# Two mixture layers on one core: the branch of rare blocks ahead of the sure ones, and the last sure blocks added to the residual by one-hot matrices

## The chip, the core and the metric

The kernel is one program on one core of a Trainium2 chip. The core has five engines that run their own instruction streams and meet at semaphores: PE multiplies matrices (PEld is its weight load), DVE and ACT do element-wise work, POOL issues indirect DMAs here, and SP issues most of the plain ones. The metric is device time in microseconds (us) of one execution, lower is better, as the median of several runs. Before the change: median 962.89 us of 3 runs (954.0, 962.89 and 962.95).

## The reference

A residual stream of 1024 tokens with 256 features goes through four layers, each an attention and a feed-forward part, each gated and added to the stream. All is fp32. The two feed-forward parts that matter are mixtures of experts. That of layer 0 takes 6 of 16 experts for each token, and adds a shared expert:

```python
probs = softmax(xf @ gate_w.T)                    # xf: [1024, 256], 16 experts
_, idx = top_k(probs + gate_b, 6)
cw = einsum('tk,tke->te', take(probs, idx), one_hot(idx, 16))
for W1, B1, W2, B2, W3, B3, c in experts:         # H = 176
    h = silu(xf @ W1.T + B1) * (xf @ W3.T + B3)
    y = y + c[:, None] * (h @ W2.T + B2)
z = silu(xf @ ws1.T + bs1) * (xf @ ws3.T + bs3) @ ws2.T + bs2
return y + z
```

Layer 3 does the like with 2 of 8 experts, 512 wide and without bias. The feed-forward part of layer 1 uses weights rounded to three values, for which a mean over the whole weight is needed first:

```python
scale = mean(abs(w))
w_q = sign(w) * (abs(w) >= scale * 0.7)           # w1 [1024, 256], w2 [256, 1024]
```

## The kernel before

The stream lies in SBUF as eight tiles of 128 rows (`stream`, `x[t]`). The parts follow one another: `attention0`, `ffn0`, `attention1`, `ffn1` and so on; a scheduler orders the instructions of each engine along the dependencies and the program's order, and an engine runs its own in that order.

**Blocks.** In `ffn0` and `ffn3` the routing sorts tokens by expert on the chip, into blocks of 128 rows that belong to one expert. The worst case has `NB0` = 63 blocks in layer 0 and `NB3` = 23 in layer 3; 55 and 20 (`SURE0`, `SURE3`) are always run, the others stand in a branch, `tc.If(used > sure)`, on a number that the routing leaves in SBUF. In the profiled execution the branch was not entered. Ahead of it, `keep_rows` (L371) writes the stream to a DRAM buffer `sums`, so that blocks can add to it there; layer 0 has two such buffers, for even and odd blocks (the second holds only what is added), layer 3 has one.

**One block**, by the lines of the profile:

- `fetch`, L1174: POOL issues an indirect DMA that gathers the block's rows, with their expert weights, from DRAM (`xd`) into `xs`. Six such tiles exist, and the gathers run four blocks ahead.
- `turn`, L1186: PE transposes the rows, DVE copies them out (L1187), DVE picks the weight of the expert (L1192), and PE's sequencer reads the offset of the expert's weights into a register (L1202, `value_load`, some three instructions).
- `up`: L1211 and L1215 in layer 0 (bias, then gate and up projection), L1226 in layer 3; ACT does the silu (L1234), DVE the product (L1235).
- `turn_hidden`: transposes on PE (L1241), copy on ACT (L1243).
- `down`, L1250: the down projection; ACT or DVE copies the result into `ring` (L1261, L1259), and POOL issues an indirect DMA (L1262) that adds the 128 rows to `sums`.

The three stages of neighbouring blocks are interleaved: step `i` turns block `i`, does `up` of `i - 1` and `down` of `i - 2`. After each step of layer 0, `between(i)` places other work: the folding of attention 1's weights (`fold1`, at every third step until it ends), then steps of `ternary1` (from step 33), which make the three-valued weights of layer 1: absolute sums on DVE (L1493), a PE sum over partitions, the threshold, and two DVE passes over each eighth of the weights (L1512, L1513).

**After the blocks** of layer 0, SP (L1403) and ACT (L1405) load both buffers back, 512 KB at a time, DVE adds them (L1408), and `attention1` begins: layernorm (L394 writes `xn`), transposes (L406), projections (L421), then softmax from L427. After layer 3's blocks, four DRAM-to-DRAM DMAs (L1662) copy `sums` to the output, two from SP and two from ACT. These are the lines around the branch and the end of layer 0:

```python
def run(self, sure):
    self.blocks(0, sure, self.between)
    used = nc.values_load(self.used, min_val=0, max_val=self.nb)
    with tc.If(used > sure):
        self.blocks(sure, self.nb, lambda i: None)
```

## Time and profile before

| what | value |
|---|---|
| median of 3 runs | 962.89 us (954.0 to 962.95) |
| the profiled execution | 967.09 us, its span 965.3 us |
| mean granted PE clock in it | 0.941 |
| PE busy | 856.9 us, 89% of the span |
| DVE, ACT, POOL busy | 509.9, 286.8, 345.7 us |
| layer 0, 272 to 451 us: PE busy | 171.44 of 179 us |
| 451 to 479 us: PE busy | 0.10 of 28 us |
| layer 3, 835 to 950 us: PE busy | 114.53 of 115 us |
| 950 to 965.3 us: PE busy | 2.13 of 15.3 us |
| scatters of layer 0 (L1262) | 55, median 1592 ns |
| gathers of layer 0 (L1174) | 55, median 987 ns |

The span runs from the first to the last instruction, and the execution's time has 1.8 us around it. A row of a group gives the line, the engine, the operation, the tile written and the tiles read, and how often; times in brackets are how long the engine had been idle and what released it. An fp32 matmul of the program appears as two records on PE. "PEq", "POOLq" and "SPq" are the sequencers, whose loads, branches and DMA issues do not count as busy time. A DMA row of POOL shows the issue alone; the data land later.

### The profile page before, as it was taken

The page shows a single profiled execution, that of the slowest core. Times are in us where ns is not written, and L with a number is a line of the kernel's source. Part 1 is how long each engine was busy: PE and PEld are TensorE (multiplying, and loading weights), DVE is VectorE, ACT ScalarE, POOL GpSimd, SP SyncE. Part 2 cuts the span into 40 slices and gives each one's busy share as a digit, 9 for nine tenths or more (in the row PEclk, how much of TensorE's full clock was granted, in tenths as well). Part 3 has the DMA queues.
Part 4 walks back from the last instruction along what each step waited for, and adds up shares of the span by engine and source line. Part 5 has one row for each costly group of instructions (what it writes and reads, how often), then busy time and mean ns, then how long its engine had stood idle before and what let it go on. Part 6 is the DMA issues. An engine that isn't in the chain of part 4 may idle for free.

```text
span 965.3 us, 12724 instructions
## 1 busy us (share of the span) xinstructions
PE 856.9 (89%) x4467; PEld 555.5 (58%) x4467; DVE 509.9 (53%) x1299; ACT 286.8 (30%) x559; POOL 345.7 (36%) x262
## 2 busy tenths in 40 slices
PE   6999999999999999986199986997867889999994
PEld 4444336876667876764046872754544556666662
DVE  4566648748624444571427755867776856222220
ACT  2122014433112322322113445415534441122221
POOL 1454543110146787786001323402311302144421
PEclk9999999999779999998599999986988999999998
DMA  9201157000256666655640000360000012122223
GB/s 364 79 21 34 61 160 200 22 22 9 84 129 158 125 141 150 121 82 63 186 174 1 1 1 0 111 227 1 1 22 1 1 44 54 43 45 45 39 23 66
DMA packets 38762, 75.15 MB, mean 78 GB/s; under 512 B 6240, under 2 KB 26706, under 8 KB 37322
## 3 DMA queue, kind: packets, MB, share of 16 engines
q1 hardware_dynamic: 23562, 52.01, 16.0%
q0 software_dynamic: 14496, 20.47, 13.1%
q10 hardware_dynamic: 640, 1.84, 0.5%
q8 instruction: 39, 0.64, 0.3%
q14 instruction: 25, 0.20, 0.1%
HBM read 58.73 MB, written 16.61 MB: 78 GB/s over the span
## 4 chain that ended last, share of the span: by engine, by line
PE 31%; DVE 10%; issue 4%; ACT 3%; POOL 2%; DMA 0%; POOLq 0%; ACTq 0%; DVEq 0%
PE wide L1226 7%; PE mm L421 5%; PE mm L1250 3%; PE wide L1436 2%; PE mm L451 2%; PE mm L656 2%; PE mm L965 2%; PE wide L923 1%; PE mm L1457 1%; DVE mx L934 1%; DVE attn L936 1%; PE mm L1637 1%; PE mm L1241 1%; DVE big L1483 1%; POOL h L1482 1%
## 5 line engine op out<-in xcount | busy, mean ns | idle before, releaser
L437 POOL TENSOR_TENSOR attn<-attn,sm 128x1024 f32<-128x1024 f32 x32 | 60.9, 1903 | 212.5 <-DVE sm L436 192.5
L1235 DVE SCALAR_TENSOR_TENSOR blk<-wide,weight,blk 128x176 f32<-128x176 f32 (+1 forms) x75 | 37.0, 493 | 135.3 <-ACT blk L1234 121.2
L1262 POOL DMA_INDIRECT sums<-ring,big x55 | 88.1, 1601 | 33.6 <-issue 10.2
L421 PE MATMUL wide<-xT,big 128*128 128x512 f32 x192 | 86.7, 600 | 0.3 <-ACT big L556 0.3
L683 DVE TENSOR_TENSOR rope<-wide,big 128x512 f32<-128x512 f32 x96 | 59.6, 683 | 47.7 <-PE wide L421 46.6
L1174 POOL DMA_INDIRECT xs<-xd,big x55 | 54.9, 999 | 63.3 <-DMA sums<-x 35.6
L1215 PE MATMUL wide<-big,blk 128*128 x220 | 77.1, 472 | 0.0
L1226 PE MATMUL wide<-big,blk 128*128 x160 | 72.2, 593 | 0.5 <-DVE blk L1187 0.5
L1234 ACT ACTIVATE blk<-wide 128x176 f32<-128x176 f32 (+1 forms) x75 | 29.4, 392 | 122.3 <-PE wide L1226 60.2
L421 PEld LDWEIGHTS wide<-xT,big 128*128 128x128 f32 x192 | 35.0, 190 | 46.7 <-issue 40.5
L656 PE MATMUL mm<-vo,attnT 128*128 128x256 f32 x256 | 59.5, 386 | 0.9 <-ACT attnT L452 0.9
L1250 PE MATMUL mm<-big,blk 88*128 x220 | 57.4, 383 | 0.6 <-ACT blk L1243 0.5
L406 PE MATMUL mm<-ident,xn 128*128 128x128 f32 x112 | 19.4, 320 | 41.6 <-DVE xn L394 35.5
L656 PEld LDWEIGHTS mm<-vo,attnT 128*128 128x128 f32 x256 | 48.0, 193 | 9.1 <-ACT attnT L452 3.1
L456 DVE SCALAR_TENSOR_TENSOR x<-mm,tg,x 128x256 f32<-128x256 f32 x48 | 22.9, 478 | 54.9 <-PE mm L656 17.3
L1250 PEld LDWEIGHTS mm<-big,blk 88*128 88x128 f32 x220 | 41.9, 192 | 16.5 <-ACT blk L1243 1.5
L452 ACT COPY attnT<-mm 128x512 f32<-128x512 f32 x64 | 35.0, 588 | 54.6 <-PE mm L451 54.3
L1215 PEld LDWEIGHTS wide<-big,blk 128*128 128x128 f32 x220 | 40.6, 196 | 13.2 <-issue 1.3
L451 PE MATMUL mm<-ident,attn 128*128 128x128 f32 x256 | 38.0, 297 | 9.9 <-POOL attn L437 9.9
L435 DVE TENSOR_REDUCE sm<-attn 128x16 f32<-128x1024 f32 x32 | 38.8, 1212 | 14.9 <-ACT attn L429 12.4
L1174 POOL DMA_INDIRECT xs<-xd,scratch x20 | 19.5, 976 | 74.6 <-PE mm L1186 53.9
L1262 POOL DMA_INDIRECT sums<-ring,scratch x20 | 31.5, 1573 | 39.3 <-ACT ring L1261 16.8
(321 smaller groups left out, 1698.6 us busy)
## 6 DMA issues: line engine op xcount, KB each, us to landing
big<-in_L_w_gate_up SPq DMA_DIRECT2D x8, 1024.0 KB
big<-in_L_w SPq DMA_DIRECT2D x4, 1408.0 KB
big<-in_L_w_down SPq DMA_DIRECT2D x8, 512.0 KB
w_L_qk<-in_L_qk SPq DMA_DIRECT2D x4, 896.0 KB
big<-in_L_w SPq DMA_DIRECT2D x4, 704.0 KB
big<-in_L_wo SPq DMA_DIRECT2D x1, 2048.0 KB
xd<-xn SPq DMA_DIRECT2D x16, 128.0 KB
sums<-x SPq DMA_DIRECT2D x16, 128.0 KB
```

The lines of the kernel that those rows point to most:

```text
L421: nc.tensor.matmul(ps, w(c), xT[:, c, :], start=(c == 0), stop=(c == 1))
L435: nc.vector.tensor_reduce(sm, e, AX.X, ALU.add)
L437: nc.gpsimd.tensor_tensor(e, e, sm.unsqueeze(2).to_broadcast([P, groups, n]), ALU.mult)
L451: nc.tensor.transpose(ps[:, i * P : (i + 1) * P], ev[:, pr * P : (pr + 1) * P], ident)
L656: nc.tensor.matmul(ps[:, :D], aT[:, s, :], vo[:, s, :], start=(s == 0), stop=(s == NP - 1))
L683: nc.vector.tensor_tensor(m[:, s, :].rearrange("q (b t) -> q b t", t=S), ps[:, s, :].rearrange("q (b t) -> q b t", t=S), table, ALU.mult,)
L1174: nc.gpsimd.indirect_dma_start(out=xs, out_offset=None, in_=self.xd, in_offset=bass.IndirectOffsetOnAxis(ap=self.gather[:, b : b + 1].bitc ...
L1215: nc.tensor.matmul(ps[:, 0, : 2 * n], st[:, c * P : (c + 1) * P], self.w[:, bass.ds(r + c * 2 * n, 2 * n)], start=False, stop=(c == 1),)
L1226: nc.tensor.matmul(ps[:, k, :n], st[:, c * P : (c + 1) * P], self.w[:, bass.ds(r + (2 * c + k) * n, n)], start=(c == 0), stop=(c == 1),)
L1235: nc.vector.scalar_tensor_tensor(s, lin, self.weight.pop(b), s, ALU.mult, ALU.mult)
L1250: nc.tensor.matmul(ps[:, :D], hT[:, j * P : (j + 1) * P], self.w[: self.chunk, bass.ds(r + j * D, D)], start=(j == 0), stop=(j == self.n - 1),
L1262: nc.gpsimd.indirect_dma_start(out=self.sums[b % len(self.sums)], out_offset=bass.IndirectOffsetOnAxis(ap=self.scatter[:, b : b + 1].bitca ...
```

## The change

- `run` fetches the first four blocks, reads `used` and stands at the branch; the rare blocks run inside it, ahead of the sure ones, with a gather buffer of their own (tag `low`). Then come the sure blocks.
- The last three blocks of layer 0 (`HOT0`) and the last two of layer 3 (`HOT3`) are not scattered. `hit` builds for each a one-hot matrix of 128 rows by 1024 tokens on DVE during the loop, and `add`, after the loop, multiplies it with the block's result on PE (eight matmuls a block, accumulated over the blocks) and adds the product to the stream in SBUF.
- `collect` loads the sums back ahead of `add`: in layer 0 four DMAs of 512 KB, all on SP, and four DVE additions; in layer 3 four DMAs of 256 KB, after which `done` writes each pair of tiles from SBUF to the output, from SP and ACT in turn. The DRAM-to-DRAM copies at the end are gone.
- The steps of `fold1` come at every fourth step of the loop from 5 on; two weight buffers (`used`) are given back at step 3 rather than before the loop; `ternary1` moves from the loop into `attention1`, between its projections, and its sums are kept behind the layernorm.

```diff
@@ -66,6 +67,7 @@
 
 NB0, NB3 = _blocks(E0, K0), _blocks(E3, K3)
 SURE0, SURE3 = 55, 20
+HOT0, HOT3 = 3, 2
 W0U = 4 * F0
 W0, W3 = W0U + 2 * D, 4 * F3 + 4 * D
 BIG = E3 * W3
@@ -832,6 +834,7 @@
 
     def attention1(gate):
         weff, wvo = kept.pop("fold1")
+        ternary = ternary1()
         qcT = latents()
         xT = [transposed(layernorm(0))]
         for g in range(NG):
@@ -841,6 +844,10 @@
                 ps = ps_mm()
                 mm2(ps, lambda c: weff[:, c, pr * P : (pr + 1) * P], xT[g])
                 evacuate(qcT[g][:, pr, :], ps)
+                if len(xT) == NG:
+                    next(ternary, None)
+        for _ in ternary:
+            pass
         latent_attend(qcT, wvo, gate)
 
 
@@ -1156,12 +1163,16 @@
     class Experts:
 
 
-        def __init__(self, route, xd, n, nb, stride, width, chunk, sums, w, bias, hTs, between):
+        def __init__(self, route, xd, n, nb, stride, width, chunk, sums, w, bias, hTs, between, rows, hot, room):
             self.gather, self.scatter, self.expert, self.offset, self.used = route
             self.xd, self.experts, self.nb, self.stride = xd, n, nb, stride
             self.width, self.chunk, self.n = width, chunk, width // chunk
             self.sums, self.w, self.bias, self.hTs = sums, w, bias, hTs
             self.between = between
+
+            self.rows, self.hot, self.room = rows, hot, room
+            self.held: list = []
+            self.hits: dict = {}
             self.ring = [sb.tile([P, 4, D], F32, tag="xT", name="ring", bufs=2) for _ in range(2)]
             self.weight: dict = {}
             self.xs: dict = {}
@@ -1170,7 +1181,9 @@
 
         def fetch(self, b):
 
-            xs = sb.tile([P, D + self.experts], F32, tag="xn", name="xs", bufs=6)
+
+            tag, bufs = ("xn", 6) if b < self.sure else ("low", 1)
+            xs = sb.tile([P, 272 if b < self.sure else 512], F32, tag=tag, name="xs", bufs=bufs)[:, : D + self.experts]
             nc.gpsimd.indirect_dma_start(
                 out=xs,
                 out_offset=None,
@@ -1232,7 +1245,7 @@
                         )
                 gate, lin = ps[:, 0, :n], ps[:, 1, :n]
             nc.scalar.activation(s, gate, AF.Silu)
-            nc.vector.scalar_tensor_tensor(s, lin, self.weight.pop(b), s, ALU.mult, ALU.mult)
+            self.weighted = nc.vector.scalar_tensor_tensor(s, lin, self.weight.pop(b), s, ALU.mult, ALU.mult)
 
         def turn_hidden(self, b):
             st, f = self.st[b], self.chunk
@@ -1259,6 +1272,9 @@
                 nc.vector.tensor_copy(y, ps[:, :D])
             else:
                 nc.scalar.copy(y, ps[:, :D])
+            if b in self.hits:
+                self.held.append((self.hits.pop(b), y))
+                return
             nc.gpsimd.indirect_dma_start(
                 out=self.sums[b % len(self.sums)],
                 out_offset=bass.IndirectOffsetOnAxis(ap=self.scatter[:, b : b + 1].bitcast(U32), axis=0),
@@ -1267,19 +1283,56 @@
                 compute_op=ALU.add,
             )
 
-        def run(self, sure):
-
-            self.blocks(0, sure, self.between)
+        def hit(self, b, room, after=None):
+
+            base, step = self.rows
+            row, at = small([P, 1], "row"), small([P, NT], "at")
+            copied = nc.vector.tensor_copy(row, self.scatter[:, b : b + 1])
+            if after is not None:
+                behind(copied, after)
+            nc.vector.tensor_scalar(at, base, row, -1.0 / step, ALU.subtract, ALU.mult)
+            for h, first in room:
+                n = h.shape[1]
+                nc.vector.tensor_tensor(
+                    h,
+                    place.unsqueeze(1).to_broadcast([P, n, P]),
+                    at[:, first : first + n].unsqueeze(2).to_broadcast([P, n, P]),
+                    ALU.is_equal,
+                )
+            return room
+
+        def add(self, held, done):
+
+            for t in range(0, NT, 2):
+                ps = ps_mm()
+                for u in (t, t + 1):
+                    for i, (hits, y) in enumerate(held):
+                        h = next(h[:, u - v, :] for h, v in hits if v <= u < v + h.shape[1])
+                        at = (u - t) * D
+                        nc.tensor.matmul(ps[:, at : at + D], h, y, start=(i == 0), stop=(i == len(held) - 1))
+                two = stream[:, t : t + 2, :]
+                nc.vector.tensor_tensor(two, ps.rearrange("p (u d) -> p u d", u=2), two, ALU.add)
+                done(t)
+
+        def run(self, sure, collect, done=lambda t: None):
+
+            self.sure = sure
+            for b in range(4):
+                self.fetch(b)
             used = nc.values_load(self.used, min_val=0, max_val=self.nb)
             with tc.If(used > sure):
-                self.blocks(sure, self.nb, lambda i: None)
-
-        def blocks(self, first, last, between):
-            for b in range(first, min(first + 4, last)):
-                self.fetch(b)
+                self.blocks(sure, self.nb, lambda i: None, 0)
+            self.blocks(0, sure, self.between, 4)
+            collect()
+            self.add(self.held, done)
+
+        def blocks(self, first, last, between, ahead):
             for i in range(first, last + 2):
-                if i + 4 < last:
-                    self.fetch(i + 4)
+                if i + ahead < last:
+                    self.fetch(i + ahead)
+                b = last - self.hot + (i - last // 2) // 5
+                if last == self.sure and i >= last // 2 and i % 5 == last // 2 % 5 and b < last:
+                    self.hits[b] = self.hit(b, self.room(b), self.weighted)
                 if i < last:
                     self.turn(i)
                 if i >= first + 2:
@@ -1370,8 +1423,6 @@
         in_three(NT, up, turn, down)
         for _ in steps:
             pass
-        used("L0_s13")
-        used("L0_s2")
         keep_rows(sums0[0], 0)
         placing = route[1]
         expert = placing[2]
@@ -1383,32 +1434,50 @@
 
         fold = fold1()
         ended = []
-        ternary = ternary1()
 
         def between(i):
-            if i % 3 == 2 and not ended:
+            if i == 3:
+                used("L0_s13")
+                used("L0_s2")
+            if i > 4 and i % 4 == 1 and not ended:
                 try:
                     next(fold)
                 except StopIteration as end:
                     ended.append(end.value)
-            if i > 32 and ended:
-                next(ternary, None)
-
-        moe = Experts(placing, xd, E0, NB0, W0, F0, FC0, sums0, big[:, : E0 * W0], (bias_0, choice), hTs, between)
-        moe.run(SURE0)
+
+        added, hits = [], []
+
+        def collect():
+
+            more = [t4([P, TPG, D], "more") for _ in range(NG)]
+            groups = [slice(g * TPG, (g + 1) * TPG) for g in range(NG)]
+            for g in range(NG):
+                nc.sync.dma_start(out=stream[:, groups[g], :], in_=tiled(sums0[0], 0)[:, groups[g], :])
+            for g in range(NG):
+                nc.sync.dma_start(out=more[g], in_=tiled(sums0[1], 0)[:, groups[g], :])
+            for t in range(0, NT, 2):
+                two, its = slice(t, t + 2), slice(t % TPG, t % TPG + 2)
+                added.append(
+                    nc.vector.tensor_tensor(stream[:, two, :], stream[:, two, :], more[t // TPG][:, its, :], ALU.add)
+                )
+
+        def room(b):
+            i = b - SURE0 + HOT0
+            if i < 2:
+                if not hits:
+                    hits.append(region("wqk", 2048, "hits"))
+                return [(hits[0][:, i * 1024 : (i + 1) * 1024].rearrange("p (t q) -> p t q", t=NT), 0)]
+            most = sb.tile([P, 768], F32, tag="hits", name="hits", bufs=1)
+            rest = sb.tile([P, 512], F32, tag="low", name="hits", bufs=1)[:, :D]
+            return [(h.rearrange("p (t q) -> p t q", q=P), t) for h, t in ((most, 0), (rest, 6))]
+
+        rows = block[:, :NT], float(NT)
+        moe = Experts(
+            placing, xd, E0, NB0, W0, F0, FC0, sums0, big[:, : E0 * W0], (bias_0, choice), hTs, between, rows, HOT0, room
+        )
+        moe.run(SURE0, collect)
         kept["fold1"] = ended[0]
-        for t in range(NT):
-            if t % TPG == 0:
-                tiles = slice(t, t + TPG)
-                nc.sync.dma_start(out=stream[:, tiles, :], in_=tiled(sums0[0], 0)[:, tiles, :])
-                more = t4([P, TPG, D], "more")
-                nc.scalar.dma_start(out=more, in_=tiled(sums0[1], 0)[:, tiles, :])
-            if t % 2 == 0:
-                two, its = slice(t, t + 2), slice(t % TPG, t % TPG + 2)
-                done = nc.vector.tensor_tensor(stream[:, two, :], stream[:, two, :], more[:, its, :], ALU.add)
-        load_experts3(0, EARLY3, done)
-        for _ in ternary:
-            pass
+        load_experts3(0, EARLY3, added[-1])
 
     def ffn3(gate):
         normal = normalised()
@@ -1468,8 +1537,39 @@
         def hTs(st, b):
             return hidden[:, (b % 4) * 512 : (b % 4 + 1) * 512]
 
-        moe = Experts(route[0], xd, E3, NB3, W3, F3, P, sums3, big, None, hTs, lambda i: None)
-        moe.run(SURE3)
+        def collect():
+            for t in range(0, NT, 2):
+                nc.sync.dma_start(out=stream[:, t : t + 2, :], in_=tiled(sums3[0], 3)[:, t : t + 2, :])
+
+        def done(t):
+            engine = nc.scalar if t % 4 else nc.sync
+            rows = slice(t * P, (t + 2) * P)
+            engine.dma_start(out=out[rows].rearrange("(t p) d -> p t d", p=P), in_=stream[:, t : t + 2, :])
+
+        hits = sb.tile([P, 2048], F32, tag="C", name="hits", bufs=C_SLOTS)
+
+        def room(b):
+            at = (b - SURE3 + HOT3) * 1024
+            return [(hits[:, at : at + 1024].rearrange("p (t q) -> p t q", t=NT), 0)]
+
+        moe = Experts(
...
+            (full, 1.0),
+            HOT3,
+            room,
+        )
+        moe.run(SURE3, collect, done)
 
 
     def ternary(k):
@@ -1490,13 +1590,14 @@
         for k in range(2):
             part = small([P, 16], "part", 2)
             for i in range(4):
-                nc.vector.tensor_reduce(
+                done = nc.vector.tensor_reduce(
                     part[:, i * 4 : (i + 1) * 4],
                     loaded[f"L1_w{k + 1}"][:, i * 512 : (i + 1) * 512].rearrange("p (a b) -> p a b", a=4),
                     AX.X,
                     ALU.add,
                     apply_absolute_value=True,
                 )
+                behind(done, kept["normal"])
                 yield
             nc.vector.tensor_reduce(sums[:, k : k + 1], part, AX.X, ALU.add)
         ps = ps_mm()
@@ -1654,12 +1755,6 @@
         if step is ffn1:
             kept["weights2"] = weights2(tg[:, 6:7])
         step(tg[:, k : k + 1])
-
-    for i in range(4):
-        rows = slice(i * T // 4, (i + 1) * T // 4)
-        to, of = (v[rows].rearrange("(p r) d -> p (r d)", r=4) for v in (out, sums3[0]))
-        engine = nc.scalar if i % 2 else nc.sync
-        engine.dma_start(out=to, in_=of)
```

## The prediction

> **What bounds the kernel now.** I read the busy table first, then the engines by stretches, then the timeline around the two places that the change cuts, then rows by source line.
>
> ```profile
> PE 856.9 (89%) x4467; PEld 555.5 (58%) x4467; DVE 509.9 (53%) x1299; ACT 286.8 (30%) x559; POOL 345.7 (36%) x262
> ```
>
> The mean says "matmul bound", so a gain must come from a stretch where PE stands still. The stretches (start:end, length, then busy time of PE, PEld, DVE, ACT, POOL; clock; DMA share) show where:
>
> ```profile
> 272.00:451.00 179.00, 171.44 (x909) 126.69 (x909) 82.18 (x282) 50.91 (x144) 131.05 (x102) 0.97 0.61 126
> 451.00:479.00 28.00, 0.10 (x1) 0.13 (x1) 6.54 (x24) 2.16 (x4) 7.58 (x5) 0.53 0.52 121
> ...
> 511.00:570.00 59.00, 55.61 (x362) 45.46 (x355) 42.55 (x64) 24.29 (x34) 16.99 (x10) 0.97 0.00 1
> ...
> 950.00:965.30 15.30, 2.13 (x10) 1.44 (x8) 0.42 (x1) 0.70 (x2) 3.10 (x2) 0.75 0.36 87
> ```
>
> PE is idle for 28 us after layer 0's blocks and for 13 us at the end. The timeline says what fills the first hole:
>
> ```profile
> 449.74 1.13 PE L1250 MATMUL mm<-big,blk 88*128 x4 [0.46 <-ACT blk L1243]
> 450.82 1.55 POOL L1262 DMA_INDIRECT sums<-ring,big  x1 [1.71 <-issue]
> ...
> 460.09 1.55 POOL L1262 DMA_INDIRECT sums<-ring,big  x1 [0.74 <-DMA sums<-ring,big]
> 465.64 0.34 SPq L1403 DMA_DIRECT2D x<-sums  x1
> ...
> 478.90 2.10 PE L406 MATMUL mm<-ident,xn 128*128 128x128 f32 x8 [28.03 <-DVE xn L394]
> ```
>
> PE finishes at 450.87, but five scatters are still queued on POOL, one per 2.3 us; the load back waits for the last (end 461.64), then come adds and a layernorm. Before that, POOL paces the stage:
>
> ```profile
> L1262 POOL DMA_INDIRECT sums<-ring,big x55: 1550/1592/1853, 281.8 to 460.1; - x55
> L1174 POOL DMA_INDIRECT xs<-xd,big x55: 952/987/1378, 256.8 to 436.6; - x55
> ```
>
> With the 0.30 us between two issues, a block costs POOL 1.60 + 0.30 + 0.99 + 0.30 = 3.19 us; PE's own cadence there is about 2.65. So three scatters fewer is worth something, but so is a late start.
>
> **The start of layer 0 (loss).** In the new program's order on PE, the `value_load`s (weight addresses) of the first ten sure blocks stand ahead of the branch, where four preceded the first block; the rare blocks' own eight are jumped over.
>
> ```profile
> L1202 PEldq TENSOR_LOAD <-big x55: 296/302/507, 270.7 to 441.9; - x55
> L1202 PEldq FUSED_REGOPS  x75: 146/151/165, 271.3 to 934.8; - x75
> L1274 PEldq COMPARE_BRANCH  x2: 233/342/450, 450.3 to 951.6; - x2
> ```
>
> The four at 270.7 came about 0.75 us apart (load, arithmetic, bounds test). Six more: 4.5. The read of `used` 0.4–0.6, compare 0.45, the step to the next instruction 0.2–0.6 (as after the old branch), semaphores about 0.5: +6.7 us for the first block. What covers this? Little: PE's shared expert runs until 271.8, and the loads stand behind it in order. POOL passes the same branch, having six gathers out; it then waits for their landing (2.2 us, as at 461.64 to 463.82), resets its counters (the 1.68 us that lie at 464.0 today) and issues four more gathers (4 x 1.29), which ends near 286, before the first result. So the first scatter moves from 281.78 to 281.78 + 6.7 = 288.5. Bounds: 0, if the loads overlap the shared expert, to 9, if POOL's wait also holds PE.
>
> The old branch, taken in the same way over the same code, shows the next event 0.2–0.6 us after the compare on every engine: no stall for code. A rule speaks against the change: the Trainium skill ("Runtime: NRT & Kernel Launch", section "Instruction fetch mechanics") says that a taken branch whose target lies outside the window already fetched holds the engine until that code has come. The trace's instruction queue q8 (39 packets, 0.3% of 16 engines' 965.3 us) gives about 1.2 us a packet, so by the rule the sum would end some 2.4 us later, one packet at each of the two branches. I follow the row.
>
> **The end of layer 0 (gain).** POOL's work from the first scatter to the last end (461.64 - 281.78 = 179.86) was 55 x 1.90 + 46 x 1.29 = 163.8, so 16.0 were waits: about 10 for results that PE brought late (largest 3.77 at 303.67), 5.4 in the tail. Now 52 x 1.90 + 45 x 1.29 = 156.9. The early waits follow PE, so I keep most; the tail, seven scatters without gathers between, keeps about 3.5: 13.5 in all. The last scatter ends at 288.5 + 156.9 + 13.5 = 458.9. Bounds: 454.7 (no late start, all waits: 281.78 + 156.9 + 16) to 461.6 (nothing gained).
>
> From that end to PE's transposes took 478.90 - 461.64 = 17.26 us. The POOL counter reset (1.68 + 0.16) goes, since no branch stands there now. The four 512 KB loads are all on SP instead of two queues; those of `sums0[0]` can start one scatter earlier, which about pays for that. All four adds stand ahead of the first layernorm on DVE in the new order; two were waited for before: +1.4 (2 x 0.69). Four additions of the one-hot product (4 x 0.69) are partly between: +1 to 2, less the better overlap of the loads. I take 17.26 - 1.84 - 0.6 = 14.8 (bounds 12 to 19). Transposes at 458.9 + 14.8 = 473.7 instead of 478.90: **-5.2**, bounds -12 to +2.
>
> The 24 one-hot matmuls (0.43–0.47 us from one to the next, two records each, as in the 128x256 fp32 rows) take 10.3–11.2 us from PE's end near 456.6, and end near 467, behind the landing and the loads. Uncovered they would cost all 11. The one-hot matrices (128x1024 on DVE, 1.13–1.22 us, with two small ones 1.5; three here, two in layer 3) lie in DVE's idle time: 82 of 179 busy in the loop; uncovered, 7.5 us. Fold steps moved to every fourth block keep their work; they lie under POOL's pace, since PE's cadence with the old spacing was below it. The six early address loads are missing from the loop later, which gains nothing under that pace.
>
> PE's clock is half from 452.4 to 483.1 today; the one-hot work may shorten this. It still idles 6 us afterwards, so I book nothing (bounds 0 to -2.1, half of 478.9–483.1).
>
> **Ternary weights moved to attention 1 (loss).** Formerly DVE did this in POOL's shadow:
>
> ```profile
> L1493 DVE TENSOR_REDUCE part<-w_L_w x8: 675/678/686, 364.9 to 388.7; 128x4 f32<-128x512 f32 x8
> L1512 DVE TENSOR_SCALAR low<-w_L_w,nthr x8: 475/480/488, 414.2 to 425.2; 128x512 f32<-128x512 f32 x8
> L1513 DVE SCALAR_TENSOR_TENSOR w_L_w<-w_L_w,thr,low x8: 741/746/752, 414.7 to 427.7; 128x512 bf16<-128x512 f32 x8
> ```
>
> Together 8 x 1.90 + 1 = 16.2 us. The stage of projections (479–511) has DVE busy 9.6 of 32, so most fits. But the threshold needs a PE matmul that stands after 18 of the last 24 projections, at about 505.5 on today's scale. Then 6.5 of the eight pairs (8.0 us) and four evacuations (2.8) stand before the first softmax maximum, with about a microsecond of steps between; 505.7 + 12.2 = 518 against today's:
>
> ```profile
> 514.56 1.23 DVE L427 TENSOR_REDUCE mx<-wide 128x16 f32<-128x1024 f32 x1 [1.23 <-PE wide L641]
> ```
>
> That is +3.5, and another 1.2 us of pairs stand before the second softmax's subtraction: **+4.5** (2.5 to 6; outer bounds 0, hidden, and 16.2, none hidden). DVE is busy 9.4 of 9.5 us there, so PE waits through.
>
> **Layer 3 start (loss).** Five `value_load`s ahead of the branch, none of them beside the first matmuls: 5 x 0.75 = 3.8, less the two that ran already (1.5), + 0.45 + 0.35 for `used` and compare: **+2.9** (2 to 4.5). PE paces this stage (5.8 us a block), so it stays.
>
> **Layer 3 end (gain).** Today:
>
> ```profile
> 952.90 0.42 DVE L1259 COPY ring<-mm 128x256 f32<-128x256 f32 x1 [3.51 <-PE mm L1250]
> 955.08 1.55 POOL L1262 DMA_INDIRECT sums<-ring,scratch  x1 [2.95 <-DMA sums<-ring,scratch]
> 958.90 1.20 SPq L1662 DMA_DIRECT2D out_dram<-sums  x2
> ```
>
> The last block's result is in SBUF at 953.3, then scatter, landing and copy until the end, 965.3: 12 us. New: 16 one-hot matmuls (6.5–7.0), of which one is ready early, evacuating add 0.7 plus steps 0.2, DMA issue 0.5 and landing 2.2, close 1.03: 11.1, so **-0.9** (-3 to +2).
>
> **Sum.** -5.2 + 4.5 + 2.9 - 0.9 = +1.3, on the profiled execution's 967.09 us (span 965.3 plus 1.8 around it): 968.4. That execution stands 4.2 above the median of 962.89; I carry the difference over: 964.2, call it 964.
>
> **Rivals.**
> *Ternary uncovered* (slower): if the threshold comes so late that all 16.2 us stand in front of softmax, the sum is -5.2 + 16.2 + 2 = +13, 976. Decides from about 13 us exposed. For: DVE is full from 514.5. Against: the eight reductions (5.4) lie in a DVE that is 70% idle.
> *Late start hidden* (faster): the last scatter ends at 454.7 and the pairs cost 1: -9.4 + 1 - 1 = -9.4 to, with the shorter half clock, -11.5: about 952. For: the loads run on PE's queue, which could run ahead of its array. Against: at 270.7 they did not.
> *The scatters save nothing* (the change does not do what it says): POOL's waits grow by what was removed, the end stays at 461.6, only the counter reset goes: -2.4 + 4.5 + 2.0 = +4: 967.
>
> **Numbers.** 1% is 9.6 us, about what a measurement here can tell from no change. Forecast 0.50, scatters save nothing 0.16, ternary uncovered or a start as bad as its upper bound 0.18, late start hidden 0.16. The forecast's own range, 957–970, covers its parts; the other cases widen it to 953–975. Within 1%: forecast, third rival and a little of the others, 0.66; slower 0.20; faster 0.14.
>
> **What would show it.** Right: the first layer-0 block near 281, 52 scatters ending near 459 with the same 3.2 us pace, transposes near 474, first softmax maximum about 3.5 us later after them than the 35.7 of today, layer 3's first block 3 us later after the shared expert, the tail from the last down-projection to the end near 11 us. Wrong: waits in POOL's chain that grow (the fold steps in other places could do it), hit matrices that wait for their space and hold DVE, or a code-fetch hole after either branch.

## The result and the profile after

The changed kernel takes 959.66 us (median of 20 runs, 954.66 to 968.39), the kernel before 961.53 us (20 runs, 954.0 to 970.67). The ratio is 0.9985 with a 95% interval of 0.9963 to 1.0006: 1.4 us by the ratio, not distinguishable from nothing. The forecast was 1.3 us slower, "within 1%": the 1% came out, and the 1.3 us lie just outside the interval.

The page of the changed kernel begins as before, with two shares that moved: PE is busier (869.7 us for 856.9; the one-hot products are 17.6 of it), POOL less (337.9 for 345.7, with five scatters fewer).

```profile
span 960.2 us, 12959 instructions
...
PE 869.7 (91%) x4544; PEld 566.6 (59%) x4547; DVE 523.0 (54%) x1323; ACT 286.6 (30%) x559; POOL 337.9 (35%) x257
```

By stretches (columns as in the prediction: busy time of PE, PEld, DVE, ACT, POOL, clock, DMA share, rate), the 28 us hole after layer 0 has become 16 us, of which the one-hot products fill 10.7; a new hole of 8 us stands ahead of the first block:

```profile
268.00:276.00 8.00, 0.41 (x2) 0.44 (x3) 0.86 (x9) 0.00 (x0) 1.47 (x2) 0.66 0.58 159
276.00:453.00 177.00, 170.09 (x908) 126.33 (x907) 71.42 (x255) 50.80 (x143) 130.31 (x100) 0.98 0.59 122
453.00:469.00 16.00, 10.68 (x50) 9.07 (x48) 7.30 (x20) 1.95 (x3) 1.54 (x1) 0.98 0.71 220
...
948.80:960.20 11.40, 6.96 (x33) 5.78 (x31) 3.19 (x5) 0.00 (x0) 0.00 (x0) 0.99 0.34 117
```

The timeline of the new hole, PE and POOL:

```profile
266.93 0.69 PE L1420 MATMUL mm<-b,cwT 18*128 18x256 f32 x2 [0.40 <-ACT cwT L1419]
...
268.86 0.62 POOL L158 DMA_DIRECT2D b<-in_L_b  x1
...
275.59 1.08 PE L1199 MATMUL mm<-ident,xs 128*128 128x128 f32 x4 [7.96 <-PEq L1323]
...
276.52 1.00 POOL L1187 DMA_INDIRECT xs<-xd,big  x1 [7.05 <-PE mm L1199]
```

"PEq L1323" is PE's sequencer at the branch. Its own rows say what it did from 267.1 to 275: ten address loads, then the read of `used` and the compare. POOL's rows at the same line show that it was late as well: it waited for its DMAs, reset its counters at 274.8 and was free at 275.1.

```profile
L1215 PEldq TENSOR_LOAD <-big x55: 295/301/677, 267.1 to 444.2; - x55
L1215 PEldq FUSED_REGOPS  x75: 146/151/165, 267.7 to 930.7; - x75
...
L1323 PEldq COMPARE_BRANCH  x2: 337/352/367, 274.6 to 827.9; - x2
L1323 POOLq INC_SWDGE_SEM  x2: 327/500/672, 274.8 to 809.4; - x2
```

The end of layer 0 and of the kernel:

```profile
452.96 10.53 PE L1312 MATMUL mm<-ring,hits 128*128 128x256 f32 x48
453.01 1.54 POOL L1278 DMA_INDIRECT sums<-ring,big  x1 [1.02 <-DMA sums<-ring,big]
...
454.54 0.83 SPq L1455 DMA_DIRECT2D x<-sums  x2
457.48 0.81 SPq L1457 DMA_DIRECT2D more<-sums  x2
461.63 2.50 DVE L1461 TENSOR_TENSOR x<-x,more 128x512 f32<-128x512 f32 x4 [10.08 <-DMA more<-sums]
...
468.81 2.21 PE L408 MATMUL mm<-ident,xn 128*128 128x128 f32 x8 [5.32 <-DVE xn L396]
...
946.86 1.99 PE L1263 MATMUL mm<-big,hidden 128*128 x8 [0.73 <-ACT hidden L1256]
948.69 7.07 PE L1312 MATMUL mm<-ring,hits 128*128 128x256 f32 x32
```

Subtracting the landmarks of the two timelines gives the account, each stretch from the end of the one above it. Forecasts are the prediction's terms.

| stretch | before, us | after, us | difference | forecast |
|---|---|---|---|---|
| start to the end of layer 0's shared expert on PE | 271.8 | 267.6 | -4.2 | 0 |
| to the start of the first scatter | 10.0 | 17.7 | +7.8 | +6.7 |
| to the end of the last scatter of layer 0 | 179.9 | 169.2 | -10.7 | -9.4 |
| to PE's transposes of attention 1 | 17.3 | 14.2 | -3.0 | -2.5 |
| to the first softmax maximum | 35.7 | 38.4 | +2.8 | +3.5, and 1.0 behind it |
| to the end of layer 3's shared expert | 319.5 | 319.4 | -0.2 | 0 |
| to the first block's projection | 0.9 | 3.6 | +2.7 | +2.9 |
| to the end of the last down projection | 117.8 | 118.7 | +0.8 | 0 |
| to the end | 12.4 | 11.4 | -1.1 | -0.9 |

The sum is -5.1, the difference of the two spans; without the first row, which lies ahead of everything that the change touches, it is -0.9.

Each trace is of one execution, and some of a row can be PE's clock: every trace has stretches in which the granted clock is 0.50, here called half clock, and they do not lie at the same places. Layer 3's +0.8 is of that kind. In the changed kernel's execution the clock is half for 3.4 us from 830.3, at the first blocks; in experiments 3, 7, 8 and 12, which have the same code there, it is not, and the stretch takes 117.0 us instead of 118.7. What the clock does to the two softmax rows is worked out in the point on the ternary weights below.

### The profile page after: what moved, and what is told of

Its sections match the earlier page's. It is cut to its first block, busy times and chain, and to the rows that moved or that the text cites. A ratio compares the mean times of both kernels' runs of the same rounds, so it can differ in the third digit from the quotient of the medians.

```text
span 960.2 us, 12959 instructions
## 1 busy us (share of the span) xinstructions
PE 869.7 (91%) x4544; PEld 566.6 (59%) x4547; DVE 523.0 (54%) x1323; ACT 286.6 (30%) x559; POOL 337.9 (35%) x257
## 3 DMA queue, kind: packets, MB, share of 16 engines
q0 software_dynamic: 13776, 19.81, 12.2%
## 5 line engine op out<-in xcount | busy, mean ns | idle before, releaser
L1278 POOL DMA_INDIRECT sums<-ring,big x52 | 83.0, 1595 | 27.8 <-issue 8.3
L423 PE MATMUL wide<-xT,big 128*128 128x512 f32 x192 | 88.7, 612 | 0.0
L1228 PEld LDWEIGHTS wide<-big,blk 128*128 128x128 f32 x220 | 40.9, 196 | 13.5 <-issue 1.3
L458 DVE SCALAR_TENSOR_TENSOR x<-mm,tg,x 128x256 f32<-128x256 f32 x48 | 23.0, 480 | 47.1 <-PE mm L972 17.1
L1239 PEld LDWEIGHTS wide<-big,blk 128*128 128x128 f32 x160 | 29.4, 194 | 30.6 <-issue 29.8
L437 DVE TENSOR_REDUCE sm<-attn 128x16 f32<-128x1024 f32 x32 | 38.8, 1212 | 14.8 <-ACT attn L431 12.3
L453 PE MATMUL mm<-ident,attn 128*128 128x128 f32 x256 | 37.2, 293 | 9.7 <-POOL attn L439 9.7
L1200 DVE COPY blk<-mm 128x256 f32<-128x256 f32 x75 | 31.3, 420 | 19.3 <-PE mm L1199 19.0
```

The lines of the kernel that those rows point to most:

```text
L423: nc.tensor.matmul(ps, w(c), xT[:, c, :], start=(c == 0), stop=(c == 1))
L437: nc.vector.tensor_reduce(sm, e, AX.X, ALU.add)
L453: nc.tensor.transpose(ps[:, i * P : (i + 1) * P], ev[:, pr * P : (pr + 1) * P], ident)
L1228: nc.tensor.matmul(ps[:, 0, : 2 * n], st[:, c * P : (c + 1) * P], self.w[:, bass.ds(r + c * 2 * n, 2 * n)], start=False, stop=(c == 1),)
L1239: nc.tensor.matmul(ps[:, k, :n], st[:, c * P : (c + 1) * P], self.w[:, bass.ds(r + (2 * c + k) * n, n)], start=(c == 0), stop=(c == 1),)
L1278: nc.gpsimd.indirect_dma_start(out=self.sums[b % len(self.sums)], out_offset=bass.IndirectOffsetOnAxis(ap=self.scatter[:, b : b + 1].bitca ...
```

## The experiments

Each is compared with the kernel before by the ratio and its interval, and with the changed kernel (0.9985) by its trace, stretch by stretch as in the table. "Changed" figures are those of the changed kernel. Nine executions have 52 scatters and a block loop that no edit slows (the changed kernel, experiments 4, 5 and 7 to 12): their chains, from first to last scatter, take 167.7 to 171.4 us, so a microsecond or two of the chain in one trace says nothing.

**1. Address loads held back, late.**

```diff
+            if 2 <= b < self.sure:
+                offset = sb.tile([1, 1], I32, tag="addr", name="addr", bufs=4)
+                behind(nc.vector.tensor_copy(offset, self.offset[0:1, b : b + 1]), self.weighted)
             self.at[b] = nc.tensor.value_load(offset, ...)
```

> The changed kernel, but each weight-address load from the third sure block on reads a copy that DVE makes only after the product of the block two before it, so two loads and not ten (layer 0) or five (layer 3) stand ahead of the branch. Theory (PE's address loads set the late start): 8 x 0.71 = 5.7 us fewer on PE in layer 0, of which POOL, free only at 275.2 in the changed kernel's trace, lets about 5 through to the first scatter; 3 x 0.68 = 2.0 us fewer in layer 3; together 7 us, ratio to the changed kernel about 0.993 (median near 953 where the changed one has 960). Rival (POOL's own wait at the branch, for its gathers to land, is as long as PE's loads and sets the first scatter): layer 0 gains under 1.5 us, total 2 to 3 us.

Measured: 972.45 us, ratio to before 1.0135 (1.009 to 1.018), slower, where faster was expected. Half of the theory shows: the first block's projection comes 3.6 us after the shared expert and not 9.2, and layer 3's 1.8 and not 3.6. The first scatter gains less, 3.5 us where about 5 were expected (14.2 after the shared expert for 17.7): POOL is free only 8.3 us after it, and four gathers stand in between, so with the loads gone the rival's wait sets the first scatter. And the chain of scatters is 178.8 us for 169.2, and layer 3's blocks take 7.2 us more. PE's groups in the loop say where (columns: busy, mean ns, idle just before, what ended it):

```profile
L1258 PE MATMUL mm<-ident,blk 128*88 128x128 f32 x96 | 19.6, 286 | 18.8 <-DVE blk L1200 9.7 <-DVE ring L1276 5.8 <-issue 1.5
```

PE stands still for 18.8 us ahead of the transposes that follow each address load, 1.6 us in the changed kernel. The load waited for a copy that came only with the product two blocks back, and kept PE's sequencer some 0.6 us more: one copy, for example, runs at 350.97 us, its load from 351.14 to 351.77, and the transposes begin at 351.83 (the row names other DVE instructions that stand beside the copies). So the experiment shows a part of the start's cause and adds a new wait of its own.

**2. The ternary weights moved alone** (in the kernel before).

```diff
-            if i > 32 and ended:
-                next(ternary, None)
...
                 evacuate(qcT[g][:, pr, :], ps)
+                if len(xT) == NG:
+                    next(ternary, None)
```

> The kernel before with one edit: the ternary weights of layer 1 are made between the projections of attention 1 as in the changed kernel, not in the block loop. Theory (their pairs delay the first softmax): the first softmax maximum comes 38 to 39 us after the first transposes of attention 1 instead of 35.7, the block loop keeps its length, the whole is 3 us slower (ratio to before 1.003). Rival 1 (DVE relieved in the loop lets POOL run closer): the last scatter of layer 0 comes 2 us or more earlier and the whole is even. Rival 2 (not covered): 10 us or more slower.

Measured: 961.6 us, ratio 1.0016 (0.999 to 1.0041), not distinguishable from even. In the trace the first softmax maximum comes 37.7 us after the transposes, 2.1 later than before, and the eighth and last one of this attention 46.8 us after the first, 1.3 later. Sign, place and size are those of the theory, 3 us, which the interval (1 us faster to 4 slower) holds as well as nothing. The chain of scatters, 178.8 us for 179.9, is no sign of rival 1.

**3. All blocks of layer 0 scattered**: `HOT0, HOT3 = 0, 2`, and no additions where nothing is held.

> The changed kernel with HOT0 = 0: all 55 sure blocks of layer 0 are scattered, no one-hot work there (layer 3 keeps its two). Theory (three scatters fewer are a gain of the POOL chain): from the first scatter to the last end about 176 us instead of the changed kernel's 169.2, the wait from there to PE's transposes about 11.5 us instead of 14.2 (four additions of 0.69 fewer), half a microsecond to 1 lost to the clock; 4 to 5 us slower than the changed kernel (ratio to it 1.0045). Rival (waits eat the scatters): even or 2 us faster than the changed kernel.

Measured: 962.31 us, ratio 1.0032 (1.0005 to 1.0059), 4.5 us above the changed kernel by the two ratios. The chain is 175.2 us: three scatters are worth 6.0 us by this pair, 4 to 7.5 by the spread of the chains. The way from there to the transposes was expected 2.7 us shorter, since four additions are gone, and is the same (14.0). The timeline says why:

```profile
457.62 1.55 POOL L1278 DMA_INDIRECT sums<-ring,big  x1 [0.45 <-issue]
459.56 0.33 SPq L1459 DMA_DIRECT2D more<-sums  x1
461.35 0.80 SPq L1457 DMA_DIRECT2D x<-sums  x2
...
467.84 1.29 DVE L1463 TENSOR_TENSOR x<-x,more 128x512 f32<-128x512 f32 x2 [16.75 <-DMA x<-sums]
```

With 55 scatters the last one goes into the first buffer (block 54), which is needed first and loaded after it; with 52 the last goes into the second (block 51), and the loads of the first start 3 us earlier (454.54 for 457.48 in the fence above). So three may be a good number for its parity too. How much that is worth is not shown apart from the spread: the first addition of loaded sums comes 8.7 us after the last scatter here, 7.1 in the changed kernel, and 6.8 to 9.9 in the eight other executions with 52 scatters and the branch in front.

**4. The branch behind the sure blocks again**, in both layers.

```diff
-            used = nc.values_load(self.used, ...)
-            with tc.If(used > sure):
-                self.blocks(sure, self.nb, lambda i: None, 0)
             self.blocks(0, sure, self.between, 4)
+            used = nc.values_load(self.used, ...)
+            with tc.If(used > sure):
+                self.blocks(sure, self.nb, lambda i: None, 0)
             collect()
```

> The changed kernel with the branch of rare blocks behind the sure ones again (ahead of the load back and of the one-hot additions), in both layers. Theory (the branch ahead costs 6.4 us at the start of layer 0 and 2.7 in layer 3, and saves only POOL's counter reset at the end): starts as in the kernel before (2.8 and 0.9 us from the shared expert's last matmul to the first block's projection), the way from the last scatter to the transposes about 2 us longer than 14.2, the end of layer 3 half to 1 us longer; 6 us faster than the changed kernel in all (ratio to it 0.994). Rival (the wait of all engines at a branch at the end is dearer than at the start): even or slower.

Measured: 956.82 us, ratio 0.9966 (0.9945 to 0.9987); against the changed kernel 2 us better, inside the noise, where 6 were expected. The starts are as the theory said: 3.2 and 0.9 us, that is 6.0 and 2.7 less. But the way from the last scatter to the transposes is 21.4 us, not 16:

```profile
446.21 1.13 PE L1262 MATMUL mm<-big,blk 88*128 x4 [0.46 <-ACT blk L1255]
451.16 12.67 PE L1311 MATMUL mm<-ring,hits 128*128 128x256 f32 x48 [3.82 <-PEq L1323]
468.45 1.88 PE L408 MATMUL mm<-ident,xn 128*128 128x128 f32 x7 [4.62 <-DVE xn L396]
```

POOL waited at the branch until its DMAs had landed and then reset its counters from 450.75 to 452.35, and SP issued the loads only behind that, at 452.4 to 454.2. The first addition of loaded sums therefore came 12.4 us after the last scatter for 7.1, which is 5.3 of the 7.2 us. PE stands 3.8 us at the branch as well, runs the one-hot products partly at half clock (12.67 us for 10.53), and ends them at 463.8, just when DVE needs the last of them: nothing covers them with time to spare any more. So in layer 0 the branch costs about as much at either end (6.0 us at the start, 7.2 here): its move is not a gain in itself, it makes room for the one-hot work to be hidden. In layer 3 it is a loss: the start gives 2.7 us back, and the end is only 0.7 longer (12.1 for 11.4).

**5. Address loads held back, early**: as in 1, but behind the product of the block four before, and with six buffers for the copies instead of four.

```diff
+                behind(nc.vector.tensor_copy(offset, self.offset[0:1, b : b + 1]), self.products[max(b - 4, 0)])
```

> The changed kernel; each address load from the third sure block on reads a copy that DVE makes after the product of the block four before it (the first three after the first product), two blocks earlier than in the experiment with late addresses. Theory (there the wait for the copy, and not the place of the load, made PE's loop longer): the first scatter comes 4 to 5 us earlier than in the changed kernel, the chain from first to last scatter stays at 169 to 171 us, layer 3 starts 1.8 us earlier and keeps its pace; 6 us faster than the changed kernel (median near 953.5). Rival (an address load that stands among the matmuls holds PE for 0.7 us wherever it is): the chain grows to 175 us or more and the whole is even or slower.

Measured: 952.37 us, ratio 0.991 (0.9877 to 0.9942), 7 us below the changed kernel, as the theory said, and the two intervals do not meet. The first projection of layer 0 follows the shared expert by 3.2 us and the first scatter by 12.5 (changed 17.7), the chain is 169.6, layer 3 starts after 1.8 and keeps its pace (117.7). But the 5.2 us at the first scatter are not all the loads' worth. In this execution the shared expert ran at half clock (its line stands in the next section), POOL's gathers ahead of the branch lay further apart, and POOL was free 6.6 us after it; at full clock it was free after 8.3 us in experiment 1 and 9.2 in experiment 9, which have the same two loads ahead of the branch, and the first scatter came after 14.2 and 15.1. PE's wait of experiment 1 is gone:

```profile
L1259 PE MATMUL mm<-ident,blk 128*88 128x128 f32 x108 | 21.4, 280 | 1.7 <-DVE addr L1219 1.6
```

**6. Ternary steps back in the loop, two blocks held**: `HOT0 = 2`, fold steps at every third step, ternary steps from 36 on, odd sums loaded first.

> The changed kernel with the ternary steps in the block loop again (from step 36) and the fold steps at every third step; since the third one-hot matrix lies in the space that the ternary steps need, HOT0 = 2, and the sums of the odd blocks are loaded first. Theory (2 to 3 us of the loss is the pairs ahead of softmax; a scatter is worth 2.3): the first softmax maximum 35.7 us after the transposes instead of 38.4, the chain of scatters 2.3 longer; even with the changed kernel within 1.5 us. Rival (DVE's work in the loop slows POOL's chain by more): 3 us or more slower.

Measured: 964.57 us, ratio 1.0041 (1.0008 to 1.0074), 5 us above the changed kernel. The softmax maximum is back at 35.5 us, 3.0 less. But the chain is 175.3 us, 4 more than one scatter (2.0 by experiment 3) explains, and the way to the transposes is 17.7, 3.4 more: 1.8 of it before the first addition, the rest because in this kernel's order DVE takes the statistics of all eight tiles ahead of the first `xn`. The rival's sum came out; experiment 12 excludes the fold steps alone as its cause. The clock is an unlikely one: this execution's loop has three half-clock stretches of 3.4 us for one in the changed kernel's, but that of experiment 12 has 6.8 us of them and a chain of 169.3. The ternary steps are the likelier cause, which is not shown.

**7. PE kept busy behind the one-hot products.**

```diff
+                    spin = ps_wide()
+                    for _ in range(12):
+                        nc.tensor.matmul(spin[:, 0, :D], h, y, start=True, stop=True)
```

> The changed kernel with 12 matmuls more behind the 24 one-hot ones of layer 0, into a PSUM tile that nobody reads (5.3 us, as long as PE's wait for the first layernorm). Theory (PE's half clock from 468.5 to 475 in the changed kernel follows its 5 us of idleness): the clock stays full there, and the first softmax maximum comes 35 to 36 us after the first transposes instead of 38.4; 2.5 us faster. Rival (the half clock has another trigger, or DVE sets that stretch): the stretch keeps its 38 us, and the whole is even or half a microsecond slower.

Measured: 961.78 us, ratio 1.0003 (0.9964 to 1.0042). The theory does not come out. The windows (PE busy, ..., clock) of the extra work, of the transposes, and of the projections after them:

```profile
455.70:471.40 15.70, 15.70 (x73) 13.50 (x72) 5.13 (x12) 1.66 (x2) 1.55 (x1) 1.00 0.64 174
473.40:476.50 3.10, 1.63 (x8) 0.90 (x8) 2.80 (x11) 0.26 (x2) 0.00 (x0) 0.98 1.07 410
477.00:483.00 6.00, 5.91 (x7) 2.52 (x8) 4.72 (x10) 0.42 (x2) 0.00 (x0) 0.50 1.07 381
```

The transposes run at full clock now, but the half clock comes all the same, later, over six microseconds in which PE is busy. From the transposes to the softmax it is 40.9 us, not 35 to 36. Idleness is not excluded as the trigger, since between the extra work and the half clock (471.4 to 476.4) PE was still busy for only 1.6 of 5 us. The way from the last scatter was 16.0 us here (changed 14.2), because the sums landed later (first addition after 8.8 us for 7.1); why, the trace does not say.

**8. The second four tiles behind the first layernorm.** The additions for tiles 4 to 7 are issued after `layernorm(0)`.

```diff
-        xT = [transposed(layernorm(0))]
+        normal = layernorm(0)
+        kept.pop("later")()          # the additions of tiles 4 to 7, behind kept["normal"]
+        xT = [transposed(normal)]
```

> The changed kernel with the additions of layer 0's second four tiles (two of the loaded sums, two of the one-hot products) behind the first four tiles' layernorm on DVE. Theory (DVE's order is what lies between the landing and the transposes): 14.25 us from the last scatter to the transposes become 12 (two additions of 0.69 and one of the products fewer ahead of them), the rest unchanged; 2 us faster than the changed kernel. Rival (the second four tiles come too late for PE, which needs them after 8 projections): what is won is given back, the first softmax maximum is 1.5 us or more later after the transposes.

Measured: 956.52 us, ratio 0.9958 (0.9926 to 0.999), about 2.5 us below the changed kernel, which the two intervals alone do not tell apart. The trace shows what the edit does: from the first addition of loaded sums to the transposes it is 5.6 us, here and in experiments 9 and 10, and 7.2 in the changed kernel and experiments 1, 5, 7 and 12. That is a gain of 1.6 us where about 2.25 were expected; 0.4 of it was lost in this execution because the sums landed later, so that the transposes come 13.1 us after the last scatter for 14.2. The softmax maximum after 37.3 us (1.1 less) is the clock's: half for 3.4 us here and 6.5 in the changed kernel's execution; experiment 4, without this edit, has 3.4 us too and 37.2. So nothing is given back, and nothing more is won.

**9. Experiments 5 and 8 together.**

> The changed kernel with both edits that won: address loads held to four blocks ahead, and the additions of the second four tiles behind the first layernorm. Theory (they act in different places): their gains of 7 and 2.5 us add up, ratio to the kernel before about 0.989. Rival (with the earlier start PE or DVE, not the landing, sets the way from the last scatter to the transposes): no better than the early addresses alone, 0.991.

Measured: 950.94 us, ratio 0.9888 (0.9843 to 0.9934), where the theory said 0.989. The interval holds the rival's 0.991 too, but the trace has both effects: the first projection 3.7 us after the shared expert (changed 9.2), layer 3 started after 1.8, and the 5.6 us of experiment 8.

**10. POOL with fewer DMAs out at the branch**, added to 9.

```diff
+            if b in (4, 5):
+                rows = sb.tile([P, 1], I32, tag="rows", name="rows", bufs=2)
+                behind(nc.vector.tensor_copy(rows, self.gather[:, b : b + 1]), self.first)
...
+        behind(kept["b2_1"], kept["scattered"])
```

> The kernel with both edits, and two more ahead of layer 0's branch: the gathers of blocks 4 and 5 read a copy of their rows that DVE makes behind the branch, and the load of a bias of layer 1 on POOL stands behind the last scatter, so that POOL has four DMAs out at the branch and not seven. Theory (POOL waits at the branch until the last of these has landed, 5.7 us after PE's last shared matmul with early addresses): the first scatter comes 10.5 us after the shared expert instead of 12.5; 1.5 to 2 us faster than with both edits, ratio to before about 0.9875. Rival (six gathers then stand ahead of the first scatter instead of four, 2.6 us more on POOL): even.

In the same edit the first two steps of the loop fetch behind `turn` and no longer ahead of it. Measured: 949.05 us, ratio 0.9866 (0.9825 to 0.9908), the lowest of all, though not distinguishable from 9. POOL's idle time at the branch is 4.7 us for 8.2, first in the kernel of 9, then in this one:

```profile
276.56 1.00 POOL L1190 DMA_INDIRECT xs<-xd,big  x1 [8.18 <-DVE own L1208]
```

```profile
270.72 0.95 POOL L1194 DMA_INDIRECT xs<-xd,rows  x1 [4.72 <-DVE own L1212]
```

The first scatter comes 12.1 us after the shared expert for 15.1 (10.5 was expected), but the way from the last scatter to the transposes is 15.5 for 13.5 in this execution, since the sums landed 2.0 later.

**11. All blocks of layer 3 scattered**: `HOT3 = 0`, and the four copies from DRAM to DRAM at the end.

> The changed kernel with HOT3 = 0 and the four copies from DRAM to DRAM at the end, as before: all 20 sure blocks of layer 3 are scattered. Theory (the end with one-hot matrices is 1.1 us shorter): from the last down projection to the end 12.0 to 12.5 us instead of 11.4, all else as in the changed kernel; 1 us slower. Rival (the branch, no longer at the end, was what made the old end long): 10.5 us or less there, and even or faster.

Measured: 957.15 us, ratio 0.9986 (0.995 to 1.0023), even with the changed kernel within the noise. The stretch itself is clear: 12.3 us from the last down projection to the end, for 11.4. Two blocks held are worth 0.9 us.

**12. Fold steps at every third step**: `i % 3 == 2` for `i % 4 == 1`.

> The changed kernel with the steps that fold attention 1's weights at every third step of the loop (5 to 35), as before, not at every fourth. Theory (they lie under POOL's pace at either spacing): the chain from first to last scatter keeps 168.5 to 171 us; even within 1.5 us. Rival (closer steps push PE above POOL's pace, which is what made the chain 175.3 with the ternary steps back in the loop): 3 us longer or more.

Measured: 958.05 us, ratio 0.9969 (0.9937 to 1.0). The chain is 169.3 us for 169.2: the spacing does nothing, as the theory said.

## Why the forecast was right, point by point

**The start of layer 0** (+6.7, measured +7.8): two waits of like length lie here, and the forecast had one. (The items named for it add up to 6.05 to 6.65; 6.7 was carried, their upper end.) PE is held by the ten address loads, 0.71 us apart, as forecast: the first block's result lies in SBUF at 284.0, 16.4 us after the shared expert. POOL was to have issued its four gathers by 286 on the old scale, 14.2 us after the shared expert and so ahead of that result; it ended them at 285.1, 17.4 after it, and the first scatter stood behind them. Its last DMAs ahead of the branch, the sixth gather and a bias load that the order had put there, were awaited for 5.3 us where 2.2 were counted, so it was free no earlier than PE, and then its gathers waited for PE's transposes. With the loads taken away POOL alone holds the first scatter (14.2 and 15.1 us after the shared expert in experiments 1 and 9); with three of its DMAs taken away too it is 12.1 (experiment 10), and 10.0 before. So of the 7.8 us the loads account for 2.6 to 3.5 by themselves and POOL's landing for about 3 more, and that the sum came so near is partly luck.

**The code behind the branch** (followed the row: no stall): PE's compare began at 274.6 and took 0.37 us; the next event on PE is at 275.1. The instruction queue carried 40 packets for 39. The rule of the Trainium skill that was weighed there ("Runtime: NRT & Kernel Launch", section "Instruction fetch mechanics") did not show in these rows; whether the branch's target lay outside the window, they do not say. But two other runs, the experiments 2 and 4, have a compare of PE at the end of layer 0 that looks like such a wait:

```profile
L1279 PEldq COMPARE_BRANCH  x2: 240/2002/3765, 446.5 to 946.2; - x2
```

```profile
L1323 PEldq COMPARE_BRANCH  x2: 365/2159/3953, 446.7 to 942.8; - x2
```

The other 26 compares of PE in the 14 traces took 0.23 to 0.45 us. In these two, 3.77 and 3.95 us, and only in these, a 16 KB packet of the instruction queue begins within the compare, 1.0 us after its start; in the kernel before, with its branch at the same place, that packet began at 447.6, ahead of the compare at 450.3. So the row that the prediction followed is one of two outcomes, and the forecast was lucky to meet it; what decides between them was not tested.

**The chain of scatters** (-9.4, measured -10.7): 52 scatters and 45 gathers as summed (156.9), waits of 12.3 us where 13.5 were kept, which is within the spread of the chains.

**To the transposes** (-2.5, measured -3.0): right in size, with one weight that may be wrong. That the first buffer's loads can start earlier was booked as just paying for the single queue; in experiment 3, without it, the stretch is as long with four additions fewer, so it may be worth about as much as they cost (2.8 us). One execution says so, and the landing of the sums varies by 3 us.

**The ternary weights** (+4.5, about +2.9 at equal clock): the mis-sized term. The rows of the pair (+2.8, and -0.2 behind it) mix it with the clock. These are the stretches from the transposes to the first softmax maximum and from there to the eighth, the last of this attention, in the kernel before, the changed kernel and experiment 11, which has the changed kernel's code up to layer 3 (the clock is the third number from the end):

```profile
478.90:514.56 35.66, 35.62 (x114) 17.45 (x115) 11.43 (x23) 8.32 (x13) 0.00 (x0) 0.94 0.44 161
514.56:560.11 45.55, 43.47 (x289) 36.13 (x288) 35.01 (x50) 18.97 (x27) 11.41 (x6) 0.96 0.00 1
```

```profile
468.81:507.24 38.43, 38.43 (x123) 18.87 (x124) 25.77 (x56) 8.61 (x14) 0.00 (x0) 0.91 0.37 135
507.24:552.39 45.15, 41.51 (x283) 33.98 (x282) 36.37 (x54) 18.98 (x27) 11.40 (x6) 1.00 0.00 1
```

```profile
467.35:504.75 37.40, 37.40 (x123) 18.55 (x124) 25.77 (x56) 8.61 (x14) 0.00 (x0) 0.94 0.38 138
504.75:551.46 46.71, 43.07 (x283) 35.06 (x282) 36.46 (x54) 18.97 (x27) 11.40 (x6) 0.96 0.00 1
```

At the clock of the kernel before (0.94 and 0.96) the moved work costs 1.7 us ahead of the first maximum, where 3.5 were forecast, and 1.2 behind it, where 1.0 were; in the changed kernel's own execution a slower clock adds 1.0 to the first stretch, and a faster one hides the second. The step that was too dear is the one behind the threshold: PE's threshold matmul came 27.6 us after the transposes (496.4), and 26.6 in experiment 5, where 26.6 were assumed; but from it to the first maximum it took 10.8 to 10.9 us, not the 12.2 that the pairs and evacuations were given.

**Layer 3** (+2.9 and -0.9, measured +2.7 and -1.1): as worked out (the items of the first add up to 3.1, not 2.9); experiments 4, 5 and 11 each undo one of them and find it.

**What no term held**: in the profiled execution of before, PE's clock was half from 254.5 to 278 us while PE worked, ahead of everything that the change touches. The last 41 records of the shared expert on PE took 17.1 us there and 9.2 at full clock in the execution of after, 7.9 less; the other way, +3.7, the changed kernel's execution was late from its first 34 us on. Together they are the -4.2 of the first row.

```profile
254.50:278.00 23.50, 22.27 (x54) 13.77 (x55) 4.72 (x22) 2.25 (x6) 8.53 (x10) 0.50 0.45 129
254.70:271.80 17.10, 16.70 (x41) 10.59 (x39) 2.30 (x9) 1.93 (x5) 5.00 (x5) 0.50 0.36 103
```

```profile
258.40:267.63 9.23, 8.83 (x41) 6.07 (x40) 2.34 (x9) 1.93 (x5) 4.99 (x5) 1.00 0.52 156
```

Of the 14 profiled executions, only one other had such a stretch at this place, that of experiment 5:

```profile
259.00:282.00 23.00, 20.04 (x49) 12.83 (x50) 5.16 (x23) 1.92 (x5) 6.57 (x7) 0.51 0.46 133
```

It comes and goes with the execution, not with the kernel, so it belongs to the spread of the medians. Leaving the first row out, the pair differs by -0.9 us and the forecast was 2.2 us too high. The ternary term is 1.6 of that, and the misses of the start (1.1 too low) and of the chain (1.3 too high) cancel by chance.

**The rivals.** "Ternary uncovered" did not come: about 3 of 16 us were exposed. "Late start hidden" did not come: the start was late in full. "The scatters save nothing" did not come: three are worth 4 to 7.5 us. "Even" is made of a gain of about 15 us and a loss of about 14, and the loss at the starts was not needed: with the address loads held back and the additions in two groups the same change is 1.1% faster than before.

## What to carry to other kernels

A branch makes every engine finish what stands ahead of it, also what the order has pulled there: look for loads of registers and for DMAs that belong to later work, and tie them to an event behind the branch, a few blocks ahead of their use. When work is taken off a queue, ask what that queue was waiting for at both ends; here a good part of the gain may have hung on which of two buffers the last scatter went to. When a profile is compared with another one, subtract landmarks stretch by stretch, set aside those that lie ahead of the change, and look for an execution with the same clock before a stretch is called longer or shorter.

## What the runs showed of the hardware

- A stretch of half clock on PE need not follow idleness: in the kernel before, 23.5 us of it, with PE busy for 22.3, begin at 254.4 after 22 us without a pause (230 to 252) and 2.4 us with 0.9 of pauses. The Trainium skill ("TensorE: Matmul & The Clock Gate", section "Part 1: The HAM clock gate") has about 3.4 us of sustained work release the clock; this row disagrees. Experiment 7's six microseconds at 0.50 begin after 15.7 us of full work, a pause of 1.9 us and 3 us of which transposes fill 1.6. What sets it off stays open.
- The registers that PE reads for addresses cost its sequencer 0.71 us each when they stand in a row (ten from 267.1 to 274.2), and POOL left a branch only when all its DMAs had landed and its counters were reset (0.33 us here, 1.68 at the old place).
- PE's compare at a branch took 0.23 to 0.45 us 26 times, and 3.77 and 3.95 us in the two cases in which a packet of the instruction queue came within it (the point on the code behind the branch).
